# A graph network with its bias row laid out in memory before the accumulating transfers read it

## The chip, the cores and the metric

The kernel runs on one core of one Trainium2 chip. The metric is the device time of one execution in microseconds (us), the median of several runs.

## The reference

128 graphs are worked one after the other. Graph g has a node array x of 128 x 512 and a weighted adjacency matrix adj of 128 x 128, all in 32-bit floats. Two layers follow each other:

```
h = relu(layernorm(x))
x = x + (hypergraph(relu_norm(hypergraph(h, adj, W1, b1)), adj, W2, b2) + h)   # layer 0
h = relu(layernorm(x))
x = x + relu(concat(h, (adj @ h) / degree) @ W.T)                             # layer 1

hypergraph(x, adj, W, b):  H = (adj != 0);  Dn, Be = inverse degrees
    return Dn * (H @ (Be * (H.T @ (x @ W.T)))) + b
```

W1 takes 512 columns to 1024, W2 takes 1024 back to 512, and W takes the 1024 columns of the concatenation to 512. What matters here is the vector b2. It has 512 elements, it is the same for all nodes of all graphs, and it is added to layer 0's result together with h and the old x.

## The kernel before, in words

A graph is one tile of 128 partitions (the nodes) by its columns. The matrix products are split into three parts (a high part, a low part and a small rest), so that each is a chain of matmuls of 128 x 512. Three arrays are too awkward to transpose on the engines alone, and go through scratch areas in memory: `inner_out` stores the 128 x 1024 result of the first convolution (the tile `r`) into `n_scratch`, and `inner_in` loads it back in four pieces as `nb`, with its 32 x 32 blocks exchanged. Layer 1's input (`h_scratch`, `hb`) and the scaled adjacency (`an_scratch`, `anb`) go the same way. The scratch pool `dram` (L73) has three buffers for each of these.

The order of all work is written out by hand: `head()` (L943) starts the first graphs and prepares the weights, `step(s)` (L855) is one turn of the steady part, called for s = 3 to 124, and `tail()` (L1216) ends the last graphs. A turn works on graphs s + 3 down to s - 4, each in another stage; each engine and each queue takes its instructions in the order in which the stages are called. Nearly all DMAs are issued on SyncE's queue (SP). The accumulating ones alone are issued by GpSimd (POOL).

Those belong to `residual(g)` (L479). It first adds H0[g] (that is h) to X[g] in two pieces on POOL (L81 by way of `combine`). Then `moved` (L90) issues a DMA with `accum_op=ADD` (L91) that adds b2, repeated for all 128 partitions, onto X[g] in on-chip memory. The reader of the result is `conv2_out(g)` (L747), three turns later: `step(s)` calls `residual(s + 1)` (L932) and `conv2_out(s - 2)` (L879). X has six buffers.

In a turn, `residual(s + 1)` is followed on POOL by `conv2_bias` of the next turn (the addition of c0 to the tile `g`, L81), and on the SP queue by `load_adj` (L859) and `inner_out` (L875). The tile `r` has one buffer. `conv1_main(s, 0)` (L873, the ScalarE instruction of L549) starts the next `r`, so it waits until the store into `n_scratch` has read the old one.

In the head, `load_bias(b1_bc, b1)` (L1010) loads the other bias onto all partitions with a DMA on SP, with `load_w2(1)` (four DMAs) behind it at L1012. The first `residual` stands at L1022.

Of the kernel before, what the change touches and what calls it, by code (L numbers as in the profile page):

```python
# [7 lines left out]
FP = mybir.dt.float32  # L8
# [16 lines left out]
def gnn_kernel(  # L25
# [32 lines left out]
    N, C, D = x.shape  # L58
    DH = w1t.shape[1]
    P = 128  # L60
# [12 lines left out]
    dram = ctx.enter_context(tc.tile_pool(name="dram", bufs=3, space=DRAM))  # L73
    psum = ctx.enter_context(tc.tile_pool(name="psum", bufs=6, space=PSUM))

    def combine(eng, dst, a, b, op):

        width = 256 if eng is nc.gpsimd else dst.shape[1]
        for c in range(0, dst.shape[1], width):
            s = slice(c, c + width)  # L80
            eng.tensor_tensor(dst[:, s], a[:, s], b[:, s], op)  # L81
# [8 lines left out]
    def moved(t, src):  # L90
        nc.gpsimd.dma_start(out=t, in_=src, accum_op=ADD)  # L91
# [16 lines left out]
    def bank(name):  # L108

        return filled(psum.tile([P, 512], FP, tag="w", name=name), FILL)  # L110
# [47 lines left out]

    b1_bc = const.tile([P, DH], FP, name="b1_bc")
    c0 = const.tile([P, D], FP, name="c0")  # L160
    gb = const.tile([P, 2, KH], FP, name="gb")
    eps = const.tile([P, 1], FP, name="eps")
    eps_root = const.tile([P, 1], FP, name="eps_root")
# [60 lines left out]
    def load_w2(half):  # L224
        src = w2t.rearrange("(j k a) o -> j a k o", j=Q, a=B)
        for j in range(Q):
            nc.sync.dma_start(out=w2[half].raw[B * j : B * (j + 1)],
                              in_=src[j, :, KD * half : KD * (half + 1)])
# [6 lines left out]
    def scale_w2(k, eng):  # L235
        t = w2[k // KD].raw[:, k % KD]
        if eng is nc.scalar:
            copy(t, t, AF.Copy, scale=vector_of(1, k))
        else:
            eng.tensor_scalar(t, t, vector_of(1, k), None, MUL)  # L240


    def load_bias(dst, src):
        nc.sync.dma_start(out=dst, in_=src.partition_broadcast(P))
# [8 lines left out]
    def vector_of(i, k):  # L253
        c = 2 * (k % 4) + k // 4
        return gb[:, i, c : c + 1]
# [5 lines left out]
    def beta_row(k):  # L261
        if not BETA:
            BETA.append(bank("pc"))
        nc.tensor.matmul(BETA[0], vector_of(0, k).to_broadcast([P, P]), w2[k // KD].raw[:, k % KD],
                         start=(k == 0), stop=(k == KH - 1))
# [5 lines left out]
    X, ADJ, ADJB, ANT = {}, {}, {}, {}  # L271
# [206 lines left out]
    @stage  # L478
    def residual(g, eng=nc.gpsimd):  # L479
        combine(eng, X[g], X[g], H0[g], ADD)  # L480
        moved(X[g], b2.partition_broadcast(P))

    @stage
    def conv1_nodes(g):
# [370 lines left out]
    def step(s):  # L855
# [74 lines left out]
        conv1_rest(s + 1)  # L930
        incidence_high(s + 2)
        residual(s + 1)  # L932
        x_spread(s + 2)
        layer1_turn(s - 2)
# [8 lines left out]
    def head():  # L943
# [64 lines left out]
        x_norm(1)  # L1008
        scale_w2(0, nc.vector)
        load_bias(b1_bc, b1)  # L1010
        beta_row(1)
        load_w2(1)  # L1012
        x_spread(2)
# [6 lines left out]
        load_adjb(3)  # L1020
        scale_w2(3, nc.scalar)
        residual(0)  # L1022
        shifts(2, 1, nc.vector)
        incidence_weight(2, nc.vector)
# [23 lines left out]
        incidence(3)  # L1048
        incidence_count(3, nc.vector)
        residual(2)  # L1050
        beta_row(6)
        w2[0].high(1)
# [462 lines left out]
    with tc.manual_schedule():  # L1515
        head()
        for s in range(3, N - 3):
            step(s)
        tail()
# [34 lines left out]
```

## Time and profile before

| what | value |
|---|---|
| median of 3 runs | 2574.51 us (2571.97 to 2574.69) |
| the profiled execution | 2573.01 us, span 2571.2 us, granted clock 0.998 |
| TensorE (PE) busy | 2497.2 us, 97% |
| VectorE (DVE) busy | 2369.4 us, 92% |
| ScalarE (ACT) busy | 2137.3 us, 83% |
| GpSimd (POOL) busy | 1256.2 us, 49% |
| DMA | 344.70 MB, mean 134 GB/s |
| the accumulating transfers | 128, 256 KB each, median 4.4 us from issue to landing |

The span runs from the first to the last instruction. "Busy" for TensorE includes modelled ends of matmuls, so 97% doesn't mean that nothing is left. A DMA-issuing instruction is not counted as busy, and its own duration is only that of the issue: the time to landing stands apart. In the page's part on DMA queues, q1 is the hardware queue (SP's), q0 the software queue (POOL's), and the last column is the time that a queue's packets took, as a share of the time of all 16 DMA engines.

### The profile page before, as it was taken

The numbers are of one execution on the slowest core, as the hardware profiler recorded it, in microseconds if no ns is written. First come the engines' busy times: TensorE is split into PE (matmuls) and PEld (weight loads), VectorE is DVE, ScalarE is ACT, GpSimd is POOL, SyncE is SP. The second block draws the span as 40 slices with busy tenths as digits, with TensorE's granted clock in tenths as the row PEclk, the third lists the DMA queues.
The fourth block names the chain that finished last, engine by engine and source line by source line (L and its number), as shares of the span: only waits on it lengthen the run. The fifth ranks groups of instructions, "written<-read, shape, count | busy, mean of one in ns | idle before, by whom it ended". The sixth has DMA issues, their size and how long they took to land.

```text
span 2571.2 us, 41753 instructions
## 1 busy us (share of the span) xinstructions
PE 2497.2 (97%) x11170; PEld 1989.8 (77%) x11170; DVE 2369.4 (92%) x5372; ACT 2137.3 (83%) x4872; POOL 1256.2 (49%) x1787
## 2 busy tenths in 40 slices
PE   8999999999999999999999999999999999999998
PEld 5777777777777777877777777777777777778776
DVE  8899999999999999999899988999999999999987
ACT  8888888888888888888888888888888888888885
POOL 4445454444444454554445444454545545544542
PEclk9999999999999999999999999999999999999999
DMA  7444444444444444444444444444444444444443
GB/s 191 130 130 131 133 130 134 134 136 128 134 136 137 128 137 134 136 131 138 128 137 131 141 130 127 133 138 132 137 129 137 133 137 130 136 136 134 130 144 96
DMA packets 427245, 344.70 MB, mean 134 GB/s; under 512 B 178688, under 2 KB 342016, under 8 KB 427008
## 3 DMA queue, kind: packets, MB, share of 16 engines
q1 hardware_dynamic: 407744, 308.40, 39.3%
q0 software_dynamic: 18688, 33.57, 8.1%
q8 instruction: 88, 1.44, 0.2%
q14 instruction: 149, 1.22, 0.1%
q10 hardware_dynamic: 576, 0.07, 0.0%
HBM read 199.50 MB, written 142.34 MB: 133 GB/s over the span
## 4 chain that ended last, share of the span: by engine, by line
PE 41%; ACT 20%; DMA 18%; DVE 11%; issue 7%; SPq 3%; POOL 0%; DVEq 0%; ACTq 0%; POOLq 0%
PE gm L529 9%; DMA n_scratch<-r 8%; DMA nb<-n_scratch 6%; PE rm L529 6%; PE bm L529 5%; PE am L529 5%; ACT r L328 3%; PE pz L487 3%; PE gd L534 3%; PE rd L534 3%; PE bd L534 3%; SPq L583 2%; PE ad L534 2%; ACT nh L611 2%; DVE nt L590 2%
## 5 line engine op out<-in xcount | busy, mean ns | idle before, releaser
L81 POOL TENSOR_TENSOR r<-r,b_bc 128x256 f32<-128x256 f32 x502 | 407.1, 832 | 522.7 <-DVE r L554 406.8
L81 POOL TENSOR_TENSOR hl<-ht,hh 128x256 fp32r<-128x256 f32 x248 | 228.3, 940 | 202.2 <-ACT hh L611 202.1
L549 ACT ACTIVATE r<-rm,dinv 128x512 f32<-128x512 f32 x256 | 174.2, 682 | 156.1 <-DMA n_scratch<-r 126.6
L302 POOL TENSOR_SCALAR st<-st 128x1 f32<-128x1 f32 x127 | 56.6, 445 | 462.2 <-DVE deg L349 449.2
L308 ACT ACTIVATE h<-x_t 128x512 f32<-128x512 f32 x255 | 159.9, 627 | 135.3 <-DVE x_t L753 128.4
L590 DVE STREAM_TRANSPOSE nt<-nb 128x1024 f32<-128x1024 f32 x127 | 158.0, 1244 | 68.0 <-DMA nb<-n_scratch 59.1
L328 ACT ACTIVATE h<-x_t,st 128x512 f32<-128x512 f32 x255 | 205.1, 804 | 0.1
L81 POOL TENSOR_TENSOR g<-g,c 128x256 f32<-128x256 f32 x246 | 201.1, 941 | 1.3 <-DVE g L693 0.6
L313 ACT ACTIVATE h<-x_t,st 128x512 f32<-128x512 f32 x255 | 184.7, 724 | 4.2
L81 POOL TENSOR_TENSOR x_t<-x_t,h 128x256 f32<-128x256 f32 x256 | 185.8, 745 | 4.7 <-ACT h L328 4.7
L554 DVE SCALAR_TENSOR_TENSOR r<-rd,dinv,r 128x512 f32<-128x512 f32 x256 | 186.0, 727 | 0.7 <-PE rd L534 0.5
L611 ACT ACTIVATE nh<-nt 128x1024 fp32r<-128x1024 f32 x127 | 134.3, 1058 | 51.5 <-DVE nt L590 50.6
L487 PEld LDWEIGHTS pz<-s,h 128*128 128x128 f32 x1024 | 126.5, 192 | 53.4 <-ACT h L328 49.3
L487 PE MATMUL pz<-s,h 128*128 128x128 f32 x1024 | 145.5, 285 | 18.9 <-ACT h L328 16.9
L328 ACT ACTIVATE r<-r,st 128x1024 f32<-128x1024 f32 x128 | 158.3, 1237 | 0.5 <-DVE st L302 0.5
L81 DVE TENSOR_TENSOR nl<-nt,nh 128x1024 fp32r<-128x1024 f32 x127 | 155.0, 1221 | 0.6 <-ACT nh L611 0.6
L620 DVE SCALAR_TENSOR_TENSOR nd<-nh,nl 128x1024 fp32r<-128x1024 f32 x127 | 154.0, 1213 | 0.0
L421 DVE TENSOR_TENSOR sb<-cnt,sb 128x2 fp32r<-128x2 f32 x128 | 143.1, 1118 | 9.3 <-ACT sb L420 5.0
L313 ACT ACTIVATE junk<-r,st 128x1024 bf16<-128x1024 f32 x128 | 147.2, 1150 | 4.2 <-DMA out_dram<-o 0.2
L529 PE MATMUL bm<-w30h,hh 128*128 128x512 f32 x504 | 147.6, 414 | 0.1
L529 PE MATMUL gm<-w20l,nl 128*128 128x512 f32 x508 | 139.9, 397 | 2.6 <-DVE nl L81 0.2
L529 PE MATMUL gm<-w20h,nh 128*128 128x512 f32 x508 | 138.6, 395 | 2.0 <-ACT nh L611 1.6
(244 smaller groups left out, 7711.3 us busy)
## 6 DMA issues: line engine op xcount, KB each, us to landing
n_scratch<-r SPq DMA_DIRECT2D x128, 512.0 KB, 4.5
nb<-n_scratch SPq DMA_DIRECT2D x508, 128.0 KB, 2.8
x_t<-in_x_dram SPq DMA_DIRECT2D x128, 256.0 KB, 2.8
x_t<-in_b_dram POOLq DMA_DIRECT2D x128, 256.0 KB, 4.4
h_scratch<-h SPq DMA_DIRECT2D x127, 256.0 KB, 2.5
hb<-h_scratch SPq DMA_DIRECT2D x508, 64.0 KB, 2.0
out_dram<-o SPq DMA_DIRECT2D x127, 256.0 KB, 2.0
adj_t<-in_adj_dram SPq DMA_DIRECT2D x128, 64.0 KB, 3.2
```

Of the source, the lines that this page charges most:

```text
L81: eng.tensor_tensor(dst[:, s], a[:, s], b[:, s], op)
L308: copy(junk, src, func, accum_out=t[:, 0:1])
L313: copy(junk, src, AF.Square, bias=t[:, 1:2], accum_out=t[:, 2:3])
L328: copy(dst, src, func, bias=t[:, 5:6], scale=t[:, 4:5])
L487: nc.tensor.matmul(z[:, k * P : (k + 1) * P], H0[g][:, k * P : (k + 1) * P], S[g], start=True, stop=True)
L529: nc.tensor.matmul(pm, left[i](k), right(i, k), start=(i == 0 and k == 0), stop=(i == 1 and k == kk - 1))
L534: nc.tensor.matmul(pd, left[2](k), right(2, k), start=(k == 0), stop=(k == kk - 1), skip_group_check=True)
L549: copy(R[g][:, HALVES[half]], PY.pop((g, half)), AF.Copy, scale=DN[g][:, 1:2])
L554: nc.vector.scalar_tensor_tensor(r, PR.pop((g, half)), dn[:, 0:1], r, MUL, ADD)
L590: nc.vector.transpose(nt.rearrange("p k (i b) -> p k i b", b=B), t.rearrange("p i k a -> p k i a"))
L611: copy(h, a, AF.Copy, scale=DOWN)
L620: nc.vector.scalar_tensor_tensor(t, h, 2.0**-12, low, MUL, SUB)
```

## The change

A scratch area `b2_rows` of 128 x 512 is allocated in memory, in the pool `dram` with one buffer. In the head a DMA on SP, between those of b1 and of the second half of W2, writes b2's row into it 128 times. Each accumulating transfer then names this area as its source, a row for each partition, in place of b2 itself repeated for each partition. The number of accumulating transfers, their place, and their bytes stay as they are.

```diff
@@ -158,6 +158,7 @@
 
     b1_bc = const.tile([P, DH], FP, name="b1_bc")
     c0 = const.tile([P, D], FP, name="c0")
+    b2_rows = dram.tile([P, D], FP, tag="b2", name="b2_scratch", bufs=1)
     gb = const.tile([P, 2, KH], FP, name="gb")
@@ -478,7 +479,7 @@
     @stage
     def residual(g, eng=nc.gpsimd):
         combine(eng, X[g], X[g], H0[g], ADD)
-        moved(X[g], b2.partition_broadcast(P))
+        moved(X[g], b2_rows)
 
@@ -1008,6 +1009,7 @@
         x_norm(1)
         scale_w2(0, nc.vector)
         load_bias(b1_bc, b1)
+        load_bias(b2_rows, b2)
         beta_row(1)
         load_w2(1)
         x_spread(2)
```

## The prediction

> **What bounds the kernel now.** I read the page first (engine shares, chain, queues, issues), then the answer on the tensor `in_b_dram` that the change concerns, the timeline of one steady turn, the waits, and last two stretches of time by engine and DMA.
>
> ```profile
> span 2571.2 us, 41753 instructions
> ...
> PE 2497.2 (97%) x11170; PEld 1989.8 (77%) x11170; DVE 2369.4 (92%) x5372; ACT 2137.3 (83%) x4872; POOL 1256.2 (49%) x1787
> ...
> PE 41%; ACT 20%; DMA 18%; DVE 11%; issue 7%; SPq 3%; POOL 0%; DVEq 0%; ACTq 0%; POOLq 0%
> ```
>
> TensorE is nearly full, but 18% of the chain is DMA, most of it the round trip of `r` through `n_scratch` (8% and 6% in the page's fourth part). So the steady part is TensorE's where a turn goes well, and the round trip's where it doesn't. The issue times of the accumulating transfers, one a turn, measure this: from the one at 84.24 us to the one at 2478.29 us there are 121 turns in 2394.05 us, 19.79 us each, while the good ones take 19.23 us and a quarter takes over 20.2 us. What DMA can give back or take is the excess over the good turn, 0.56 x 121 = 68 us.
>
> The answer on `in_b_dram`:
>
> ```profile
> L91 POOL DMA_DIRECT2D x_t<-in_b_dram x128: 895/906/967, 20.4 to 2535.0; - x128
> L244 SPq DMA_DIRECT2D b_bc<-in_b_dram x1: 352/352/352, 15.0 to 15.0; - x1
> ...
> who waited for it (us, times):
> busy tenths in 40 slices 0000000000000000000000000000000000000000
> DMA to landing us min/median/max: 4.0/4.4/6.1
> ```
>
> Nobody waits for the accumulated tile: the list of waiters is empty, since its reader comes three turns (59 us) after a landing of at most 6.1 us; the last graph's is issued at 2535.0 us and read on VectorE at 2553.4 us. The transfer matters only through what it stands in front of. One turn of the timeline:
>
> ```profile
> 1017.47 0.90 POOL L91 DMA_DIRECT2D x_t<-in_b_dram  x1 [0.30 <-POOL x_t L81]
> ...
> 1018.26 1.57 POOL L81 TENSOR_TENSOR g<-g,c 128x256 f32<-128x256 f32 x2
> ...
> 1018.52 0.38 SPq L575 DMA_DIRECT2D n_scratch<-r  x1
> ...
> 1020.15 0.61 ACT L705 ACTIVATE gp<-g 128x512 fp32r<-128x512 f32 x1
> ...
> 1023.00 0.69 ACT L549 ACTIVATE r<-rm,dinv 128x512 f32<-128x512 f32 x1 [1.03 <-DMA n_scratch<-r]
> ...
> 1023.59 0.81 ACT L328 ACTIVATE h<-x_t,st 128x512 f32<-128x512 f32 x1
> ```
>
> The store of `r` goes out 1.05 us after the accumulate, and its landing holds ScalarE, which holds `x_norm` and so TensorE's `pz`:
>
> ```profile
> ACT r L549 <- DMA n_scratch<-r: 126.6, 95, 2.7
> ...
> PEld pz L487 <- ACT h L328: 49.3, 90, 3.5
> ```
>
> In the trace's packet records the store's first packet starts 2.06 us after its issue, against 0.6 to 0.9 us for the stores of `h` and `o`: it queues behind the accumulate. A straight line of mine through 114 turns (length of the turn against the end of the store's last packet) rises by 0.84 us a us. So the price of the change in the steady part is 0.84 x 121 = 101 us for each us by which the accumulate's transfer gets longer or shorter, for shortening until the 68 us are used up. No change (5.1 us) means less than 0.05 us of a transfer.
>
> **What the skill says.** *DMA: Bandwidth & Descriptors*, "Issuing engines are not separate DMA queues": all queues run on the same 16 engines and interleave. The 2.06 us agree. The same page, "SDMA does more than copy": the accumulate is an elementwise reduce of two streams, so each packet must read the source and also the destination. This trace agrees:
>
> ```profile
> 17.30:18.60 1.30, 1.30 (x6) 1.03 (x5) 1.27 (x4) 0.60 (x3) 1.30 (x2) 0.79 1.05 419
> 1019.20:1020.50 1.30, 1.30 (x7) 0.97 (x6) 1.30 (x3) 1.27 (x6) 0.64 (x1) 1.00 0.99 172
> ```
>
> The last two columns are the DMA engines' busy share and GB/s. In the first stretch the other bias b1, also one row repeated 128 times, is loaded plainly; in the second an accumulate runs nearly alone. Both fill the engines, and the accumulate moves 0.41 of the bytes. *DMA: Bandwidth & Descriptors*, "Rules for kernel authors", allows a repeated source and warns only of a leading zero-stride dimension under 16; here it is 128, and the page's 18688 packets over 128 transfers are 146, that is 128 rows of 2 KB, 16 counts and two others. No page says what it costs that 16 engines read one row of memory.
>
> **The change part by part.**
>
> *Removed: 128 reads of one row in each transfer. Added: 128 reads of separate rows.* This is the whole steady part. The packet records give for the accumulate's 2 KB packets a median of 178 ns (5% to 50% lie between 176 and 178); a plain 2 KB packet takes 84, a plain 4 KB one 159. Two plain reads are 168, so the packet is what an engine needs to take in 4 KB, and nothing is left for a queue at the shared row. The b1 load says the same: its 4 KB packets, from one row, take 159, just as the store of `r` from on-chip memory does. Separate rows are no slower once they run: the loads of `x`, 128 rows of 2 KB one after the other, settle at 84. Both sources exceed what the accumulate can take, so I take 0 us for a transfer. The bounds: above, the x load's first three packets an engine take 254, 164 and 107 ns on the mean, 273 ns over the settled rate, where the accumulate's first three are 115 over its own; if the start-up belongs to separate rows, a transfer gains 0.16 us and the kernel 16 us. Below, the accumulate's mean packet is 197 ns, 19 over its median; if all of that came from the shared row, 8 packets an engine save 0.15 us, and the kernel 15 us.
>
> *The issue on POOL* stays 0.906 us, for the same 128 rows. It is covered: the addition behind it ends at 1019.83 us and ScalarE takes its result at 1020.15 us. The first 0.32 us of a longer issue cost nothing, each 0.1 us beyond it up to 12 us. I take 0, as the form of the transfer is unchanged.
>
> *The wait.* Each accumulate now also depends on the fill of `b2_rows`, but POOL has to wait only once, at the first (20.44 us). I put the new DMA's issue at 16.27 us: SP's DMAs take turns on 8 semaphores, each waits for the one eight before it, and the first load of W2's second half now goes out there as its predecessor landed. By that load's landing, 4.94 us, the area is ready at 21.2 us, so POOL waits 0.8 us. Behind it stands the count of graph 2 (21.13 us), which VectorE wants at 25.43 us: hidden, with 3 us to spare.
>
> *The issue on SP* (0.35 us) moves everything behind it by one semaphore: W2's four loads by 0.5 to 1.1 us, then four blocks of adj, x of graph 3 (21.23 to 22.3 us), adj of graph 0 (22.26 to 23.6 us) and four loads of the third weight (1.1 us). That x landed at 27.1 us and is read at 35.3 us. W2's last piece lands at 24.64 us now and TensorE reads it at 25.93 us; with the shift and the fill's own 256 KB on the engines (0.7 us at 84 ns a packet) it comes at 25.8 to 26.4 us. I take 0.4 us, between 0 and 1.
>
> Sum: 2571.2 us span + 0.4 = 2571.6, with 1.8 us around the span 2573.4 us for this execution, which lies 1.5 us under the median: 2574.9, say 2575 us.
>
> **The rivals.**
>
> *Faster: the single row is a hot spot.* For it: the mean packet is above the median, and the first of each engine takes 257 ns. Against it: adj's and the store's packets share the engines just then, undisturbed transfers start at 186 ns, and b1's load has no such tail. At 0.15 us a transfer, 15 us: 2560 us. At its most, if the source read cost nothing (8 x 94 ns), the 68 us would be used up: 2507 us.
>
> *Slower: reading separate rows starts slowly*, as x does. For it: the 273 ns. Against it: x comes right behind 128-byte blocks of adj, and adj's own row loads, which start in quiet, show 33 ns against 27. It decides from 0.05 us a transfer, when the store of `r` loses what the turn doesn't forgive. At 0.16 us: 2591 us.
>
> *Hidden anyway*: a gain or loss in the transfer doesn't reach the store. Against it is the slope of 0.84; for it, that the quickest turns don't move at all. It ends at 2575 us too and adds to the forecast's chance.
>
> That the change doesn't do what it says, relieve memory, is my forecast itself.
>
> **How the numbers follow.** No change: 0.48 (hidden included), own range 2570 to 2580 us. Faster by the row: 0.27. Slower by the start: 0.25. 0.2% is about what can be told from no change. The range takes both rivals' worked-out times: 2559 to 2591 us; what lies outside is the deep part of the hot spot and a POOL issue longer than its cover.
>
> **What would show it.** If right: the accumulate lands at 4.4 us again, packets at 176 to 178 ns; ScalarE's wait for `n_scratch` near 126.6 us; POOL's issue near 906 ns; bytes read almost the same (199.5 MB). Hot spot: landing under 4.25 us, that wait down by tens of us, more turns at 19.23 us. Slow start: landing over 4.5 us and the wait up. I would be wrong if POOL's issue changes by over 0.3 us, or if another scratch area's move in memory slows `nb`.

## The result and the profile after

The changed kernel took 2567.38 us (median of 7 runs, 2562.73 to 2574.43) where the kernel before took 2574.51 us. The ratio is 0.9978, with a 95% interval of 0.9962 to 0.9994: faster by 0.22%, some 6 us, just beyond the 0.2% that the prediction called no change. Three later comparisons, on three chips, gave 0.9921, 1.0003 and 0.9937 for the same program; they stand below.

The profiled execution of the changed kernel took 2574.43 us, the longest of its seven. It shows what became of each operation, but not the gain. Two lines of the page of before:

```profile
q0 software_dynamic: 18688, 33.57, 8.1%
...
n_scratch<-r SPq DMA_DIRECT2D x128, 512.0 KB, 4.5
```

The same and more from its own page (shares of the chain, the queue, the landing of the store):

```profile
span 2572.7 us, 41754 instructions
...
PE 36%; ACT 21%; DMA 21%; DVE 12%; issue 7%; SPq 3%; DVEq 0%; POOL 0%; ACTq 0%; POOLq 0%
...
q0 software_dynamic: 18688, 33.57, 9.3%
...
n_scratch<-r SPq DMA_DIRECT2D x128, 512.0 KB, 4.6
```

The accumulating queue q0 moves the same 33.57 MB in the same 18688 packets, and its packets take 9.3% of the engines' time where they took 8.1%. The answer on the new scratch area (its two issues, what their engine waited for with us and times, and the time to landing):

```profile
L91 POOL DMA_DIRECT2D x_t<-b_scratch x128: 892/906/967, 21.3 to 2536.1; - x128
L245 SPq DMA_DIRECT2D b_scratch<-in_b_dram x1: 598/598/598, 16.3 to 16.3; - x1
...
  DMA b_scratch<-in_b_dram: 0.8, 1
...
DMA to landing us min/median/max: 4.0/4.4/5.4
```

POOL's issue is unchanged at 906 ns, the fill goes out at 16.3 us, and POOL waits for it once, for 0.8 us. The median landing is 4.4 us as before. The waits behind the store of `r`:

```profile
ACT r L550 <- DMA n_scratch<-r: 128.2, 97, 2.9
...
PEld pz L488 <- ACT h L329: 51.3, 93, 3.5
```

They were 126.6 and 49.3 us before: in this execution the chain stands about where it stood.

To find what a quicker execution does otherwise, the following table is worked out from the packet records of the traces; all are means over the turns. The records don't name the engine of a packet, but each transfer ends with 16 packets of 4 bytes, which are taken here as one for each of the 16 DMA engines: "first" and "last engine" are the ends of the first and the last of them, counted from POOL's issue. "Start" is the mean duration of the first sixteen of its 2 KB packets, about one an engine. "Store" is the end of the last packet of the store of `r`, counted from its own issue. The last column is the time of that execution.

| kernel | start, ns | first engine, us | last engine, us | store, us | this execution, us |
|---|---|---|---|---|---|
| before | 257 | 3.20 | 4.13 | 4.14 | 2573.01 |
| changed, first | 464 | 3.55 | 4.14 | 4.16 | 2574.43 |
| changed, `after_again` | 356 | 3.38 | 3.96 | 3.99 | 2541.82 |
| changed, `after_third` | 318 | 3.44 | 4.09 | 4.15 | 2566.89 |
| changed, `after_fourth` | 362 | 3.42 | 3.99 | 4.01 | 2554.67 |
| `fill_only` | 250 | 3.19 | 4.16 | 4.21 | 2562.81 |
| `w2_rows` | 365 | 3.39 | 3.92 | 3.98 | 2550.06 |
| `near_rows` | 289 | 3.41 | 4.00 | 4.07 | 2548.92 |
| `onchip_source` | 183 | 3.03 | 3.29 | 3.37 | 2512.89 |
| `no_accumulate` | | | | 2.42 | 2448.61 |

Two things change with separate rows. The first packets take longer, so that the first engine is done later, and the engines finish closer together: 0.59 us apart in the first profile and 0.58 in `after_again`, where the single row has 0.93 us. The end of the store of `r` goes with the last of them throughout the table. Where the last engine ends sooner, at 3.96 and 3.99 us, the execution is quicker; where the slow start uses most or all of that up, it is not. In the first profile the start is the slowest of the four. In `after_third` the first sixteen packets are the quickest of the four, but the slow start lasts longer: the third sixteen take 288 ns there, and 207 to 209 in the other three.

### The profile page after: what moved, and what is told of

It reads as the page before. It is cut to its first block, busy times and chain, and to the rows that moved or that the text cites. A ratio compares the mean times of both kernels' runs of the same rounds, so it can differ in the third digit from the quotient of the medians.

```text
span 2572.7 us, 41754 instructions
## 1 busy us (share of the span) xinstructions
PE 2497.8 (97%) x11170; PEld 1993.5 (77%) x11170; DVE 2371.4 (92%) x5372; ACT 2138.2 (83%) x4872; POOL 1260.0 (49%) x1787
## 3 DMA queue, kind: packets, MB, share of 16 engines
q0 software_dynamic: 18688, 33.57, 9.3%
## 4 chain that ended last, share of the span: by engine, by line
PE 36%; ACT 21%; DMA 21%; DVE 12%; issue 7%; SPq 3%; DVEq 0%; POOL 0%; ACTq 0%; POOLq 0%
DMA n_scratch<-r 11%; PE gm L530 9%; DMA nb<-n_scratch 6%; PE bm L530 5%; PE am L530 5%; ACT r L329 4%; PE rm L530 3%; PE pz L488 3%; PE bd L535 3%; PE ad L535 2%; ACT h L309 2%; SPq L584 2%; ACT nh L612 2%; DVE nt L591 2%; ACT junk L314 2%
## 5 line engine op out<-in xcount | busy, mean ns | idle before, releaser
L530 PE MATMUL rm<-w11h,z 128*128 128x512 f32 x512 | 140.2, 395 | 0.0
```

The lines of the kernel that those rows point to most:

```text
L530: nc.tensor.matmul(pm, left[i](k), right(i, k), start=(i == 0 and k == 0), stop=(i == 1 and k == kk - 1))
```

## The experiments

Each was timed beside the kernel before on the same chip. The first four ran on one chip, the next four on a second, then a third and a fourth. Where a profile is set against that of the kernel before, the latter is the one of the first comparison, whose chip isn't on record.

**The changed kernel again** (no edit).

> The changed kernel once more, to see how firm 0.9978 is. Theory A (the source: the accumulates read separate rows and the store of r behind them is disturbed less) and theory B (the place: the fill in the head, or the scratch areas moved by 256 KB in memory, makes it) both expect 0.9978 again, 2566 to 2570 us. Theory C (no effect, the first comparison was chance) expects 0.999 to 1.001.

Measured: 0.9921 (0.9898 to 0.9944), 2544.29 us against 2565.67. The chain, two waits and two landings of its profile:

```profile
PE 54%; ACT 17%; DMA 13%; DVE 8%; issue 6%; SPq 2%; DVEq 0%; POOL 0%; ACTq 0%; POOLq 0%
...
ACT r L550 <- DMA n_scratch<-r: 96.4, 87, 2.1
...
PEld pz L488 <- ACT h L329: 36.4, 75, 3.5
...
n_scratch<-r SPq DMA_DIRECT2D x128, 512.0 KB, 4.4
...
x_t<-b_scratch POOLq DMA_DIRECT2D x128, 256.0 KB, 4.2
```

Against the page of before the accumulate lands 0.2 us sooner and the store 0.1 us, ScalarE waits 30 us less for the store, TensorE's weight loads 13 us less for ScalarE, and DMA's share of the chain falls from 18% to 13%. It is faster, and by more than in the first comparison: none of the three theories had expected more than 0.3%.

**The fill without the separate rows.**

```diff
 (on the changed kernel)
-        moved(X[g], b2_rows)
+        moved(X[g], b2.partition_broadcast(P))
```

> b2_rows is allocated and filled in the head as in the change, but the accumulates read b2's single row as before; the result is the same. Theory A expects the time of before plus about 1 us for the head, ratio 1.000. Theory B expects the changed kernel's time, 0.998. Theory C expects 1.000.

Measured: 0.9976 (0.9967 to 0.9985). This fits theory B in size, but on this chip it is less than a third of the changed kernel's gain, and its store ends at 4.21 us, no sooner than before. So the fill and its place are not what shortened the store. But 0.9976 is also the size of the first comparison's 0.9978, so that one alone can't be put down to the separate rows.

**Separate rows without the fill.**

```diff
 (on the kernel before)
-        moved(X[g], b2.partition_broadcast(P))
+        moved(X[g], w2t[0:P])
```

> The kernel before, but each accumulate reads 128 separate rows that lie in memory already, the first 128 rows of W2 transposed (a contiguous 256 KB, as b2_rows is), so there is no fill, no new scratch area and no new semaphore turn. It leaves out b2 and adds W2's rows in its place. Theory A expects the changed kernel's gain without its head, 0.997 to 0.998, and packets that start at 370 ns as in the changed kernel. Theories B and C expect 1.000.

Measured: 0.9946 (0.9929 to 0.9964). With no new area and no new DMA the store ends at 3.98 us, as in the changed kernel, and the start of 365 ns is there too. Separate rows alone make the larger part of the gain.

**No accumulate.**

```diff
-        moved(X[g], b2.partition_broadcast(P))
```

> The kernel before without the accumulating transfers: b2's addition is left out. This measures the price that the forecast used. By the slope of 0.84 us for each us, the store of r starts about 1.3 us sooner and all 68 us over the good turn are won: about 2507 us, ratio 0.974. If the transfer is hidden anyway, the ratio is above 0.995.

Measured: 0.9543 (0.9526 to 0.9560), 2448.47 us. That is 117 us, far more than my cap of 68. Chain and landing:

```profile
PE 97%; ACT 2%; DMA 0%; DVE 0%; issue 0%; SPq 0%; POOL 0%; ACTq 0%; DVEq 0%
...
n_scratch<-r SPq DMA_DIRECT2D x128, 512.0 KB, 2.7
```

The round trip leaves the chain altogether, and the mean turn goes from 19.80 to 18.77 us. So the 19.23 us of the good turn were no floor of TensorE: they held some of the accumulate's cost as well. The store ends 1.72 us sooner than in the profile before, so it cost 117 / 1.72 = 68 us for each us.

This run takes POOL's issue of 0.9 us out as well, and that could be a cause of its own. The profile of before speaks against it. The work behind the issue on POOL is the addition to `g`, and ScalarE waited for it once in the whole execution:

```profile
ACT gp L705 <- POOL g L81: 1.1, 1, 1.1
```

**Separate rows, on a second chip** (as `w2_rows`).

> The run w2_rows once more, in the company of the next ones; b2 is left out and W2's rows are added in its place. If the gain of separate rows holds (it was 0.9946): 0.993 to 0.997, and the accumulate's last engine again ends 0.2 us sooner than with one row. If it was chance: 0.999 to 1.001.

Measured: 0.9979 (0.9969 to 0.9990). The last engine ends at 3.93 us, the store at 4.03. The direction holds, but the gain is smaller than was expected.

**Rows that overlap.**

```diff
-        moved(X[g], b2.partition_broadcast(P))
+        moved(X[g], bass.AP(w2t.tensor, w2t.offset, [[16, P], [1, D]]))
```

> As w2_rows_2, but the 128 source rows begin only 64 bytes apart, so that they overlap and lie in 10 KB in place of 256 KB; b2 is left out and parts of W2 are added in its place. If the gain comes from spreading the reads over memory, this is near the one row: 0.999 to 1.001, early engines done at 3.2 us after the issue. If it comes from the form of the source (a step over zero, other descriptors), it is like w2_rows_2: 0.994 to 0.996, early engines done at 3.4 us.

Measured: 0.9983 (0.9970 to 0.9996), not to be told from `w2_rows_2`. Its records lie between the kinds: early engines end at 3.41 us like those of separate rows, the last at 4.00 us, between 3.93 and the 4.05 to 4.16 of a single row. It doesn't decide whether the spread over memory or the form of the source counts.

**The area alone, and one small DMA alone.**

```diff
 (alloc_only)
+    b2_rows = dram.tile([P, D], FP, tag="b2", name="b2_scratch", bufs=1)
 (small_dma)
+    b2_row = dram.tile([1, D], FP, tag="b2", name="b2_scratch", bufs=1)
...
+        nc.sync.dma_start(out=b2_row, in_=b2.partition_broadcast(1))
```

> The kernel before with the scratch area of 256 KB allocated and never used, so that at most the other scratch areas lie elsewhere in memory. If fill_only's 0.9976 comes from the place of the areas: 0.997 to 0.998. If from the DMA in the head, or from chance: 1.000.

> The kernel before with one more DMA in the head at the fill's place, of one row of 2 KB into a scratch area that nobody reads: everything behind it on SP moves by one semaphore, as in the change, without the fill's traffic. If fill_only's 0.9976 comes from this move: 0.997 to 0.998. If it comes from the 256 KB in memory, or from chance: 1.000, with at most 1 us from the head.

Measured: 0.9991 (0.9980 to 1.0002) and 1.0016 (1.0008 to 1.0024). Neither gives `fill_only`'s 0.9976 again, though the interval of the area alone comes close. That a DMA of 2 KB which nobody reads gives 0.16% is a warning: programs that differ in next to nothing differ by this much here.

**The changed kernel, the fill and a source on the chip, on a third chip.**

```diff
 (onchip_source, on the kernel before)
-        moved(X[g], b2.partition_broadcast(P))
+        moved(X[g], b1_bc[:, :D])
```

> The changed kernel a third time, on the chip of the next runs. Where separate rows let the accumulate's last engine end sooner: 0.992 to 0.998, and in the profile the store of r ends 4.0 us after its issue; an execution in which it ends at 4.15 us should show no gain. If the gain belongs to single chips: 0.999 to 1.001.

> Allocated and filled, but the single row is read. It was 0.9976; the area alone gave 0.9991 and one more small DMA 1.0016. If what is left besides the source is only the scatter between programs whose DMAs and addresses lie a little differently: anything from 0.997 to 1.002, with the store of r ending 4.1 to 4.2 us after its issue as before. If the fill itself gives something: 0.9976 again.

> The kernel before with a source that needs no read of memory: the first half of the bias b1, which lies on the chip on all 128 partitions. It leaves out b2 and adds b1's half. If the single row is slow to read from memory, this is the best of the sources: under 0.995, packets at 178 ns from the first on. If it is the quick start of the first engines that holds up the last ones, this starts at least as quickly as the single row, its last engine ends at 4.05 to 4.2 us after the issue, and the ratio is 0.999 to 1.002.

Measured: the changed kernel 1.0003 (0.9991 to 1.0014), the fill alone 0.9984 (0.9973 to 0.9996), the source on the chip 0.9795 (0.9774 to 0.9816), which is 52 us. The changed kernel has no gain here, and its store ends at 4.15 us; with the fill alone it ends at 4.05 us, a little sooner than was expected. The on-chip source is the run that settles whether the source's place matters. Its chain and landings:

```profile
PE 67%; ACT 9%; DMA 8%; DVE 8%; issue 5%; SPq 2%; DVEq 0%; POOL 0%; ACTq 0%; POOLq 0%
...
n_scratch<-r SPq DMA_DIRECT2D x128, 512.0 KB, 3.9
...
x_t<-b_bc POOLq DMA_DIRECT2D x128, 256.0 KB, 3.6
```

The median packet takes 178 ns here as with all other sources, yet the transfer lasts 1.72 us from its first packet to its last, where it lasted 2.41 us from the single row. The engines end within 0.27 us of each other, not 0.93. So most of the spread goes with reading the source from memory, and the expectation that a quick start holds up the last engine falls: this source starts quickest and ends soonest. The store ends 0.77 us sooner than in the profile before; at 68 us for each us that is the 52 us measured. The run also takes 33.55 MB of reads off memory (199.50 to 165.95). The next run speaks against that as the cause of the gain: it keeps all these reads and is faster still.

**The accumulate moved behind the store.**

```diff
     def residual(g, eng=nc.gpsimd):
         combine(eng, X[g], X[g], H0[g], ADD)
-        moved(X[g], b2.partition_broadcast(P))
+        if not 4 <= g <= N - 4:
+            moved(X[g], b2.partition_broadcast(P))
+
+    @stage
+    def bias_row(g):
+        if 4 <= g <= N - 4:
+            moved(X[g], b2.partition_broadcast(P))
...
         conv1_bias(s, 0)
+        bias_row(s)
```

> The kernel before with b2's single row, but in the steady part the accumulating DMA of graph s is issued after the second bias addition of the next turn, some 13 us after its old place and well behind the store of r; the result is the same. If the accumulate costs what it does because it stands before the store of r: the store lands in 2.7 us as it does without accumulates, and most of the 117 us come back, ratio 0.955 to 0.97. If it only moves the queue before the transfers of h: 0.98 to 1.00, and waits for hb or h_scratch appear.

Measured: 0.9589 (0.9568 to 0.9609), 2458.70 us. The chain, the waits for the two stores and for `hb`, and the landings:

```profile
PE 90%; DMA 3%; ACT 3%; DVE 2%; issue 1%; SPq 1%; POOL 0%; DVEq 0%; ACTq 0%; POOLq 0%
...
ACT r L555 <- DMA n_scratch<-r: 20.6, 29, 1.7
...
ACT g L695 <- DMA h_scratch<-h: 8.3, 11, 1.6
...
DVE ht L596 <- DMA hb<-h_scratch: 5.8, 14, 1.3
...
n_scratch<-r SPq DMA_DIRECT2D x128, 512.0 KB, 2.7
...
x_t<-in_b_dram POOLq DMA_DIRECT2D x128, 256.0 KB, 5.2
...
hb<-h_scratch SPq DMA_DIRECT2D x508, 64.0 KB, 2.6
```

The accumulate itself now lands later (5.2 us) and `hb` takes 2.6 us in place of 2.0, but these have room: in the whole execution VectorE waits 5.8 us for `hb` and ScalarE 8.3 us for the store of `h` (1.3 and 3.9 us before). ScalarE's wait for the store falls from 126.6 to 20.6 us. Of the 117 us without accumulates, 105 come back with all the work still done. POOL still issues every accumulate, only later in the turn.

**No change at all, and the source on a fourth chip.** `before_copy` is the kernel before, unchanged; `late_rows` is the changed kernel with the move of `late_accumulate`.

> The kernel before, unchanged, as if it were a change: what the comparison says of no change at all. If its interval can be trusted, 0.999 to 1.001; a ratio away from 1 by 0.002 would mean that the small differences of the other runs cannot be read.

> The changed kernel on the chip of before_copy and w2_rows_3. If its gain goes with the chip, it and w2_rows_3 agree within 0.001. If b2_rows is the worse place, this stays at 0.998 to 1.000 while w2_rows_3 is at 0.994 to 0.998. In the profile the end of the store of r (4.0 us after its issue with the gain, 4.15 without) goes with the time.

> The kernel before with the first 128 rows of W2 as source; b2 is left out and W2's rows are added in its place. 0.994 to 0.998 if separate rows help on each chip; as after_fourth if the chip decides.

> The changed kernel with the accumulate moved behind the store of r, as in late_accumulate (0.9589 with the single row). If the source matters only through what stands behind the accumulate, this is 0.957 to 0.961, as late_accumulate is; if separate rows load the engines or memory more, slower than 0.962.

Measured: no change 0.9991 (0.9979 to 1.0004), the changed kernel 0.9937 (0.9919 to 0.9956), W2's rows 0.9946 (0.9929 to 0.9963), the changed kernel with the move 0.9581 (0.9564 to 0.9598), 2458.43 us. A program against itself is within its interval of 1, and the programs that read the single row in the old place gave 0.9976 to 1.0016, so 0.994 is a gain. `b2_rows` and W2's rows agree within 0.001, as they would if the chip, and not the area, decided the size; one chip doesn't show that. And once nothing urgent stands behind the accumulate, whether it reads one row or separate rows makes no difference that can be told: 0.9581 and 0.9589, on two chips, with overlapping intervals.

## Why the prediction was wrong

**What failed is the step "Removed: 128 reads of one row, Added: 128 reads of separate rows", which took 0 us for a transfer.** I argued from the duration of one packet: 178 ns is what an engine needs to take in 4 KB, so nothing is left for a queue at the shared row. The median duration of a packet is right, and it is the same with every source. It leaves out when the packets start, and how far the slow ones set an engine back. Eight packets an engine, started 157 ns apart (the commonest distance in the records), are 1.26 us; the transfer takes 2.41 us from its first packet to its last. Of the other 1.15 us, 0.69 are gone with the source on the chip (1.72 us), so they come from the read in memory; the remaining 0.46 us weren't explained. In place of 0 us, the change moved the end of the accumulate's last engine from 4.13 us to 4.14, 3.96, 4.09 and 3.99 us in its four profiles; with the single row it lay between 4.05 and 4.16 us, so two of the four are clearly sooner. I had the records of before, and looked at how long the packets were and not at how far apart the engines ended. The stretch that I showed with the engines 99% busy began 0.1 us after the first packet and stopped 0.8 us before the last one's end, which hid the late finish.

The first comparison doesn't show this by itself: its profile has the last engine no sooner, and its 0.9978 is within what `fill_only` gives without separate rows. The later runs show it, three of the changed kernel and three of W2's rows: four of these six, 0.9921 to 0.9946, lie well below every program with the single row in the old place (0.9976 to 1.0016), and with the accumulate moved behind the store the difference between the sources is gone. That 2567.38 us lies between 2559 and 2591 us is owed to the room that the range left for the rivals, not to the step.

**Both rivals on the steady part were half right.** The slow start of separate rows is there: 464 ns against 257 in the first pair of profiles. So is a cost of the single row, though not where I looked for it. Separate rows have the longer packets on the mean (212 to 232 ns in the changed kernel, 201 with the single row), and still the last engine ends no later: the single row's cost is in the spread between the engines. The two work against each other. On balance the last engine ends up to 0.2 us sooner, or not at all sooner. I had priced "faster" at 0.15 us a transfer and 2560 us; the changed kernel's four ratios put its gain at -1 to 20 us.

**The cap was too low, and the price is known only roughly.** I had 101 us for each us of the store's end, and at most 68 us. Without accumulates it was 68 us for each us and 117 us in all. A straight line through 15 profiled executions, of all kernels here in which the accumulate stands in its old place (2513 to 2574 us), gives 71 us for each us of the store's end, with a correlation of 0.90. The on-chip source lies far from the rest and sets this slope: without it the other 14 give 111 us, with a correlation of 0.79. So the runs don't say which of these prices holds for a small shift, and my 101 us is among them. The cap took the quickest common turn for TensorE's own.

**What was right.** The chain from the accumulate by way of the store to ScalarE and TensorE is confirmed by `no_accumulate` and `late_accumulate`; the rival *hidden anyway* falls. The fill went out at 16.3 us for my 16.27, POOL waited 0.8 us once, and its issue stayed at 906 ns. The fill's own issue took 0.6 us, not 0.35. The store of `r` of graph 0 went from 33.41 to 34.05 us, 0.6 us for my 0.4.

**What stays open.** Why reading one row from memory sets the engines some 0.9 us apart, and why rows that overlap in 10 KB lie between, wasn't found. Nor was the size from chip to chip: 0.9978, 0.9921, 1.0003 and 0.9937. The profiled executions of the first comparison and of `after_third` show the same end of the store as before and no gain, those of `after_again` and `after_fourth` a sooner end and a gain. So the gain goes with the end of the store, but the price leaves part of it open: 0.15 and 0.13 us sooner are 11 and 9 us at 71 us for each us, 17 and 15 us at 111, where the ratios stand for 20 and 16 us. What makes the start slow in one and less so in another was not tried. And `fill_only` gave 0.9976 and 0.9984 with nothing in its profile to show for it, beside 0.9991 and 1.0016 for its parts. I can only set it beside the scatter between programs.

## What to carry to other kernels

For a transfer over many DMA engines, read from its first packet to the end of its last engine, not only the duration of a packet: here the end of the store behind it went with the last engine, while the median packet took 178 ns with every source. A transfer that nobody waits for can still be dear by where it is issued: moving this one behind the store gave 0.959, where other rows in memory gave 0.992 to 1.000 and a source on the chip 0.980. A floor that is taken from the quickest turns of a kernel holds only while the thing in question isn't in those turns too; leaving that thing out measures it.

## What the runs showed of the hardware

An accumulating transfer of 256 KB onto the chip lands in 3.6 us when its source lies on the chip and in 4.4 us when it is one row in memory, at the same median of 178 ns a packet. Reading it from memory cost this kernel 52 us of 2564. Its 16 engines end 0.93 us apart with one row in memory, 0.58 us with separate rows (`after_again`) and 0.27 us with the source on the chip. A store of 512 KB issued 1.2 us on the mean behind the accumulate landed in 4.5 us, and in 2.7 us without it.
